# Two layers of attention and a 3x3 convolution: where the positions enter the first attention's scores, when the folded weights are made, and who writes the picture's border

## The chip, the cores and the metric

The kernel runs on one core of a Trainium2 chip. The core has five engines with queues of their own: PE (TensorE: matmuls, with PEld for its weight loads), DVE (VectorE), ACT (ScalarE), POOL (GpSimd) and SP (SyncE, which here only issues transfers). Each engine works through its own instructions in order, and waits where an instruction needs something of another engine. The metric is the device time of one execution in microseconds (us); lower is better.

## The reference, cut to what matters

Two images of 256 channels and 64x64 pixels go through two residual layers, each behind a group normalisation. The first layer is 8-head attention over all 4096 pixels. The second has two attentions over blocks of 64 pixels (`_sa`: one over the 64 pixels that have the same place in their 8x8 blocks, then one within each block), and a 3x3 convolution of mixtures of q, k and v.

```python
x = x + _L0_conv_ref(_gn(x), qkv_w, qkv_b, 8)      # softmax(q k / sqrt(32)) v, 8 heads of 32, N = 4096
x = x + _L1_conv_ref(_gn(x), ...)
...
q = _c1x1(x, conv1_w, conv1_b)
k = _c1x1(x, conv2_w, conv2_b)
v = _c1x1(x, conv3_w, conv3_b)
loc = jnp.stack([linspace over w, linspace over h])
pos = jnp.tile(_c1x1(loc, convp_w, convp_b), (1, HEAD, 1, 1))
fq = q * float(hd) ** (-0.5) + pos
fk = k + pos
...
att = jax.nn.softmax(jnp.einsum('bcn,bcm->bnm', qf, kf) * C ** (-0.5), axis=-1)      # in _sa
...
f_conv = f_all.transpose(0, 2, 1, 3).reshape(b, hd * KC * KC, h, w)
out_conv = lax.conv_general_dilated(f_conv, dep_w, (1, 1), ((1, 1), (1, 1)), feature_group_count=hd, ...)
return rate1 * out_att + rate2 * out_conv
```

The queries and keys of the second layer's first attention are linear in the normalised image and in the pixel's place (its two coordinates and the constant 1). Their scores are therefore a sum of four products: image with image, image with place, place with image, place with place.

## The kernel before

For each image `b` the program runs: load of x, `group_stats`, `project0` (the first layer's projections), `attention0`, `layer1_first` (the second layer's first attention) and `layer1_second` (its second attention and the 3x3). N = 4096 pixels are cut into NT = 8 tiles of T = 512; the 256 channels are KC = 2 halves of 128 partitions.

At the start SP issues the eight loads of x (L70), and behind them 16 loads that put the weights w1 and w2 of the second layer in order of their output channels (`by_out`, L87), and `place_rows` (L91), the four rows of the places' weights. POOL meanwhile issues the loads of the constants, of the first layer's weights (L100 to L135) and of `grid` (L208). `group_stats` takes the statistics with VectorE (L326, L330), and two small matmuls `pm_l` and `pv_l` (L333, L343) spread them over the channels; the first projection `p_wk` (L418) needs them.

`fold_scores` (L213) runs for image 0 behind `project0`. It transposes `place_rows` to `place` (L227), multiplies w1 by w2 to the one matrix `g` of the scores (L238) so that only one projection, y, is needed for queries and keys together, and makes `pos_rows` (rows that add the query's and the key's places to y) and `w_at` (two columns that give, for each pixel, its products with the two coordinates of the key's place).

`attention0` runs through 16 groups of heads and rows in a hand-written order of PE, ACT and DVE: scores (L511), exp (L517), product with the values (L527), sums (L564). Tasks can be hung into it at a group and a step. In image 0's attention nine of them, the list `later`, split the position rows and each tile's places into two parts of reduced precision (`split`: a copy by ACT, L170, and a subtraction by DVE, L171), and store the parts to a DRAM scratch, `loc_kept`.

`layer1_first` regroups the normalised image into `xg`, with tiles in the order of the first small attention. `project` makes `py` with two matmuls for each of 2 x 8 tiles (L1136) and a third of 16 rows that adds the places (L1140); ACT writes the sum to y. `at_grid` makes `pa`, the pixels' products with the coordinates, for four tiles at a time: eight matmuls with `w_at` (L1152) and four with the places (L1154); ACT copies them to `ats` (L1157). `open_pair` loads the places of two tiles from `loc_kept` (L1118). `group_attention` then runs for each tile: `scores` (the products of xg with y, L1031, and a third one of two rows, `ats` with `grid`, L1037), the values (L1013, two halves, written by ACT or DVE), softmax by DVE and ACT (L1045 to L1052), transposes `at` (L1057), copies to a block diagonal `bd` by DVE (L1066), and the output `pc` (L1075), which ACT writes to `feats` (L1086). PE's order here is written by hand: while tile t's scores and values run, tile t-1's softmax is under way, and its `at` and `pc` follow between the halves of the projection of tile t+2. For t of 6 and 7 there is no projection left to lie between.

For image 0, `conv_weights` (L870 to L890) makes the 3x3's weights from the reference's small ones, on VectorE alone, after the first attention's regrouping (`issue_after(done)`): two halves m of 9 taps x 12 combinations (L872) and sums (L876 to L883, the last of them the last weight), each half stored by SP to `wf_kept` (L885). `fetch_conv_weights` loads them as `wf` (L900), and PE transposes them (`pw`, L909).

`layer1_second` pads the picture to 66x66 in `xp`: POOL clears the border (top row L1242, bottom row L1243, left and right columns L1244), and ACT writes the normalised image into the middle (L1248). POOL makes the 3x3's inputs from it in the Winograd form (`conv_transform`: `col` L936 and `v` L940), PE multiplies them (`mm`, L950), and between these steps run the second small attention's `branch` (`phq`, L1290, `prq`, L1298, with ACT's L1086) and `group_attention`.

Of the kernel before, what the change touches and what calls it, by code (L numbers as in the profile page):

```python
# [40 lines left out]
def direct_layers(ctx: ExitStack, tc: tile.TileContext, a: dict, out: bass.AP, bad: bass.AP):  # L41
# [35 lines left out]
    x_first = load_x(0)  # L77
# [13 lines left out]
    nc.sync.dma_start(out=place_rows, in_=a["posq"])  # L91

# [48 lines left out]
    def load_layer1():  # L141
        for name in ("fq2", "fk2"):
            wts[name] = load_const("wt_" + name, [P, KC, C], a[name].rearrange("(k p) m -> p k m", p=P))
        wts["b3"] = load_const("b3", [P, KC], a["b3"].rearrange("(k p) -> p k", p=P))
        wts["rate1"] = load_const("rate1", [P, 1], a["rate1"].partition_broadcast(P))
        wts["rate2"] = load_const("rate2", [P, 1], a["rate2"].partition_broadcast(P))
        def stack(name, rows):
            wts[name] = const.tile([16, rows.shape[1]], F32R, name="st_" + name)
            pair, second = split(rows, name)

            def rest():
                second()
                for g in range(4):
                    nc.sync.dma_start(
                        out=wts[name][4 * g : 4 * g + 4].bitcast(F32), in_=pair[:, g % 2, :].bitcast(F32)
                    )

            return rest

        later.append(lambda: (lambda: stack("pos", wts["pos_rows"])))  # L160


    later = []

    def split(rows, nm):


        n, cols = rows.shape
        pair = w4([n, 2, cols], f"pair_{nm}", F32R)
        nc.scalar.copy(pair[:, 0, :], rows)  # L170
        return pair, lambda: nc.vector.tensor_sub(pair[:, 1, :], rows, pair[:, 0, :].bitcast(F32))  # L171
# [13 lines left out]
    loc_kept = dram.tile([2, 2, 4, N], F32, name="loc_kept")  # L185

    def stack_positions(t):
        n = slice(t * T, (t + 1) * T)
        loc = w4([4, T], f"loc_{t}")
        nc.sync.dma_start(out=loc, in_=a["loc"][:, n])  # L190

        def halves_of():
            pair, second = split(loc, f"loc_{t}")

            def rest():
                second()
                for d in range(2):
                    nc.sync.dma_start(out=loc_kept[:, d, :, n].rearrange("l r n -> r l n"), in_=pair.bitcast(F32))

            return rest  # L200

        return halves_of


    grid = const.tile([P, 64], F32, name="grid")
    nc.gpsimd.memset(grid, 0.0)
    for u in range(4):
        nc.gpsimd.dma_start(out=grid[HD0 * u : HD0 * u + 2, :], in_=a["loc"][1:3, 0:64])  # L208

# [3 lines left out]
    def fold_scores():  # L213
# [3 lines left out]
        rows = w4([4, C + HD0], "pos_rows")  # L217
        wts["pos_rows"] = rows
        nc.gpsimd.memset(rows, 0.0)

        scale = const.tile([4, 1], F32, name="pos_scale")
        nc.gpsimd.memset(scale, 8.0)
        nc.gpsimd.memset(scale[0:1, :], 1.0)
# [5 lines left out]
        pl = bank([4, C + 2], "pt_rows")  # L229
        for dst, src in ((pl[:, 0:C], by_out["w2"]), (pl[:, C : C + 2], place[:, :, 1:3])):  # L230
            for j in range(KC):
                nc.tensor.matmul(dst, place[:, j, :], src[:, j, :], start=j == 0, stop=j == KC - 1)
        nc.scalar.activation(rows[:, 0 : C + 2], pl, AF.Copy, scale=scale)
        for k in range(KC):
            pg = bank([P, C + 2], f"pt_g_{k}")
            for dst, src in ((pg[:, 0:C], by_out["w2"]), (pg[:, C : C + 2], place[:, :, 1:3])):
                for j in range(KC):
                    nc.tensor.matmul(  # L238
                        dst, by_out["w1"][:, j, k * P : (k + 1) * P], src[:, j, :], start=j == 0, stop=j == KC - 1
                    )  # L240
            nc.scalar.copy(wts["g"][:, k, :], pg[:, 0:C])
            nc.scalar.copy(w_at[:, k, 0:2], pg[:, C : C + 2])
# [227 lines left out]
    def attention0(b, xts, held):  # L470
# [253 lines left out]
        rests = {}  # L724
        for n, begin in enumerate(later):
            at_block(1 + n // 2, 3 + 12 * (n % 2), lambda n=n, begin=begin: rests.update({n: begin()}))
            at_block(1 + n // 2, 8 + 12 * (n % 2), lambda n=n: rests.update({n: rests[n]()}))
            at_block(1 + n // 2, 12 + 12 * (n % 2), lambda n=n: rests.pop(n)())
        later.clear()

# [81 lines left out]
    def conv_weights():  # L812
# [49 lines left out]
        for m in range(2):  # L862
# [16 lines left out]
            for r, row in enumerate((g[0], one, two, g[2])):  # L879
# [3 lines left out]
                nc.vector.tensor_add(one, one, row[:, 1, :])  # L883
# [117 lines left out]
    def group_attention(nm, q, k, tokens, wv, out, busy=False, apart=False, more=None):  # L1001
# [25 lines left out]
        for t in range(4):  # L1027
# [7 lines left out]
            for par in range(2 if more else 0):  # L1035
                n0 = (4 * par + t) * 64
                nc.tensor.matmul(  # L1037
                    sp[64 * par : 64 * par + 64, t, :], more[0][:, n0 : n0 + 64], more[1], start=False, stop=True
                )
        if not first:  # L1040
# [50 lines left out]
    def layer1_first(b, xts, put, check, st):  # L1091
# [19 lines left out]
        tiles, banks, locs = {}, {}, {}  # L1111
# [3 lines left out]

        def open_pair(i):
            loc = w4([16, 2, T], f"loc_{b}_{i}", F32R)
            nc.sync.dma_start(  # L1118
                out=loc.bitcast(F32).rearrange("r s n -> r (s n)"),
                in_=loc_kept[:, :, :, 2 * i * T : (2 * i + 2) * T].rearrange("l d r n -> (l d r) n"),  # L1120
            )
            locs[i] = loc

        def loc_of(t):
            return locs[t // 2][:, t % 2, :]
# [813 lines left out]
```

## Time and profile before

| What | us |
|---|---|
| median of three executions (3153.34, 3155.56, 3158.25) | 3155.56 |
| the profiled execution, its own time | 3162.76 |
| its span | 3160.8 |
| start to the first projection (p_wk) | 21.0 |
| projections of image 0, and the fold, to the first scores | 21.0 to 110.5 |
| attention of image 0, to the writing of its last rows | 110.5 to 1153.7 |
| attention of image 1, from its first scores | 1698.1 to 2739.2 |
| second layer of image 0, to the first pw | to 1349.3 |
| second layer of image 1, to its first phq | to 2871.8 |

The profile is of one execution, the one of 3162.76 us in the table. In its lines an instruction group has its start, its duration, the engine (SPq is SP's queue), the line of the code, the operation, the tile written and the tiles read, and in brackets how long the engine had been idle and what ended that. Over the whole span the mean clock that PE was granted is 0.99 of full speed.

### The profile page before, as it was taken

How to read it: one execution, taken by the hardware profiler on the slowest of the kernel's cores; microseconds unless marked ns; L12 is line 12 of the kernel's file. 1: busy time of each engine (PE TensorE's matmuls, PEld its weight loads, DVE VectorE, ACT ScalarE, POOL GpSimd, SP SyncE). 2: the span in 40 equal slices, each digit the busy share in tenths (PEclk: the TensorE clock that was granted, in tenths of full speed). 3: DMA queues.
4: the chain of work that ended last, by engine and by line, in shares of the span. 5: the costliest groups of instructions: out<-in, count | busy, mean ns of one | idle time of the engine just before them, and what ended most of it. 6: DMA issues, size and time to landing. Idle time of an engine off the chain costs nothing. (4 is left out here: it accounts for less than half of the span.)

```text
span 3160.8 us, 62690 instructions
## 1 busy us (share of the span) xinstructions
PE 3059.0 (97%) x25107; PEld 1835.6 (58%) x25107; DVE 2479.1 (78%) x3203; ACT 2302.7 (73%) x2356; POOL 864.9 (27%) x933
## 2 busy tenths in 40 slices
PE   7999999999999999799999999999999999999998
PEld 4455555555555556477654555555555555466765
DVE  4599998999999998846545899899999999824543
ACT  2699999999999973432235999999999999734232
POOL 2122222222322230435301222222222222305530
PEclk9999999999999999899999999999999999999999
DMA  7968778688796661121059686786878975600000
GB/s 257 270 126 171 152 160 179 137 174 167 160 191 134 135 135 49 60 98 36 27 187 271 127 184 141 154 177 143 171 166 164 184 150 125 161 1 8 21 14 22
DMA packets 242709, 425.74 MB, mean 135 GB/s; under 512 B 99164, under 2 KB 109984, under 8 KB 239976
## 3 DMA queue, kind: packets, MB, share of 16 engines
q0 software_dynamic: 96240, 240.41, 38.2%
q1 hardware_dynamic: 146168, 181.24, 20.5%
q8 instruction: 199, 3.26, 0.4%
q14 instruction: 102, 0.84, 0.1%
HBM read 118.52 MB, written 68.12 MB: 59 GB/s over the span
## 5 line engine op out<-in xcount | busy, mean ns | idle before, releaser
L564 DVE TENSOR_TENSOR e<-e,es 128x1024 f32<-128x1024 f32 (+1 forms) x952 | 1035.9, 1143 | 91.4 <-ACT es L517 90.0
L527 PE MATMUL av<-es,v 128*32 128x256 f32 (+1 forms) x9644 | 747.6, 390 | 0.0
L564 DVE TENSOR_TENSOR e<-e,v 128x1024 f32<-128x1024 f32 (+1 forms) x640 | 676.6, 1109 | 51.2 <-ACT v L517 49.8
L517 ACT ACTIVATE es<-sa 128x1536 f32<-128x1536 f32 (+1 forms) x444 | 635.6, 1432 | 97.7 <-PE sa L511 55.0
L511 PE MATMUL sa<-q,k 128*128 128x512 f32 x1736 | 561.6, 431 | 13.6 <-ACT es L517 6.4
L527 PE MATMUL av<-v 128*32 128x256 f32 (+1 forms) x6228 | 507.9, 390 | 0.0
L527 PEld LDWEIGHTS av<-es,v 128*32 128x32 f32 x9644 | 317.0, 110 | 299.9 <-issue 162.1
L511 PEld LDWEIGHTS sa<-q,k 128*128 128x128 f32 x1736 | 280.4, 188 | 296.5 <-issue 138.3
L511 PE MATMUL sc<-q,k 128*128 128x512 f32 x1180 | 372.5, 397 | 4.3 <-ACT es L517 3.3
L511 PE MATMUL sb<-q,k 128*128 128x512 f32 x1180 | 371.2, 396 | 0.8 <-ACT es L517 0.8
L527 PEld LDWEIGHTS av<-v 128*32 128x32 f32 x6228 | 217.5, 110 | 179.4 <-issue 82.7
L517 ACT ACTIVATE es<-sc 128x1024 f32<-128x1024 f32 x296 | 306.8, 1037 | 2.6 <-DMA v<-es 2.6
L517 ACT ACTIVATE v<-sc 128x1024 f32<-128x1024 f32 x294 | 304.8, 1037 | 0.0
L517 ACT ACTIVATE es<-sb 128x1024 f32<-128x1024 f32 x296 | 302.0, 1020 | 2.4 <-DMA acc<-es 2.4
L517 ACT ACTIVATE v<-sb 128x1024 f32<-128x1024 f32 x294 | 299.8, 1020 | 0.0
L511 PEld LDWEIGHTS sc<-q,k 128*128 128x128 f32 x1180 | 211.2, 188 | 74.2 <-ACT es L517 13.1
L511 PEld LDWEIGHTS sb<-q,k 128*128 128x128 f32 x1180 | 221.3, 188 | 55.3 <-ACT es L517 2.8
L574 POOL DMA_DIRECT2D es<-es x118 | 100.7, 853 | 496.3 <-ACT es L517 450.7
L517 ACT ACTIVATE v<-sa 128x1536 f32<-128x1536 f32 (+1 forms) x146 | 209.2, 1433 | 35.3 <-PE sa L511 15.3
L950 PE MATMUL mm<-v,wf 128*128 128x256 f32 x1024 | 229.3, 383 | 4.1 <-DVE z L959 4.1
L940 POOL TENSOR_TENSOR v<-col 128x512 f32<-128x512 f32 x128 | 162.5, 1297 | 228.6 <-PE mm L950 44.0
L950 PEld LDWEIGHTS mm<-v,wf 128*128 128x128 f32 x1024 | 194.9, 191 | 39.4 <-issue 13.5
(258 smaller groups left out, 3240.6 us busy)
## 6 DMA issues: line engine op xcount, KB each, us to landing
acc<-es POOLq DMA_DIRECT2D x130, 512.0 KB, 6.1
acc<-v POOLq DMA_DIRECT2D x84, 512.0 KB, 6.1
es<-es POOLq DMA_DIRECT2D x138, 256.0 KB, 4.0
v<-es POOLq DMA_DIRECT2D x134, 256.0 KB, 4.8
k<-wk_halves SPq DMA_DIRECT2D x64, 512.0 KB
q<-wq_halves SPq DMA_DIRECT2D x256, 128.0 KB
v<-v POOLq DMA_DIRECT2D x90, 256.0 KB, 4.9
es<-v POOLq DMA_DIRECT2D x86, 256.0 KB, 3.8
```

The lines of the kernel that those rows point to most:

```text
L511: nc.tensor.matmul(sc[:, i, :], held["k", g // 2][:, j * P : (j + 1) * P], held["q", g, u // 2][:, u % 2, :], start=True, stop=True,)
L517: nc.scalar.activation(dst, sc[:, i : i + m, :], AF.Exp, scale=SC0)
L527: nc.tensor.matmul(dst[HD0 * u : HD0 * u + HD0, n], lhs, rhs(u)[:, n], start=start, stop=stop)
L564: nc.vector.tensor_add(dst[:, s, :], dst[:, s, :], src)
L574: nc.gpsimd.dma_start(out=dst, in_=src, accum_op=ALU.add)
L940: (nc.gpsimd.tensor_add if plus else nc.gpsimd.tensor_sub)(dst, rows(one), rows(two))
L950: nc.tensor.matmul(mm[:, m, r, :], wf[:, k, 4 * r + q, m * P : (m + 1) * P], v[r // 2][:, r % 2, k, :], start=k == 0, stop=k == KC - 1,)
```

## The change

Five things are changed.

1. The places become three more rows of the scores' third product. `fold_scores` now also makes `query_part` (the three weights of the query's place), `meet` (their product with the key's place), `at_key` (`meet` with `grid`) and a `w_at` of five columns. The third product has five rows for each tile: `queries`, which holds the pixels' products and the raw rows of places, and `keys`, which holds the grid's part and the products with the query's place. `queries` is laid out once in SBUF (`at_query`, cleared by POOL, with eight loads by POOL), stored to `kept_at` by SP, and loaded for each image. `at_grid` loses its four matmuls with the places, and writes with two VectorE combinations instead of ACT's copy. `project` loses its third matmul, and the nine tasks, `loc_kept` and `open_pair` go.
2. `by_out` and `place_rows` are loaded ahead of x, and `fold_scores` runs ahead of `group_stats`.
3. In `group_attention` of the first attention, for t of 6 and 7, the values run after a pause: PE's order is scores(t), at(t-1), values(t), pc(t-1).
4. In `branch` of the first tile the four matmuls run both output halves of the first input half, then those of the second.
5. For image 0 the top row of the picture's border is written by VectorE, issued after the last weight of `conv_weights`. The bottom row and the columns, and image 1's border, stay with POOL.

```diff
-    x_first = load_x(0)
...
     place_rows = const.tile([4, C], F32, name="place_rows")
     nc.sync.dma_start(out=place_rows, in_=a["posq"])
+    x_first = load_x(0)
...
-        later.append(lambda: (lambda: stack("pos", wts["pos_rows"])))
...
-    loc_kept = dram.tile([2, 2, 4, N], F32, name="loc_kept")
-    def stack_positions(t):
...
-    grid = const.tile([P, 64], F32, name="grid")
-    nc.gpsimd.memset(grid, 0.0)
+    AT = 5
+    kept_at = dram.tile([P, 2, T], F32, name="kept_at")
+    at_query = w4([P, 2, T], "at_query")
+    nc.gpsimd.memset(at_query, 0.0)
+    masks = const.tile([P, 2], F32, name="masks")
+    nc.gpsimd.memset(masks, 0.0)
+    grid = const.tile([2, 64], F32, name="grid")
+    nc.gpsimd.dma_start(out=grid, in_=a["loc"][1:3, 0:64])
     for u in range(4):
-        nc.gpsimd.dma_start(out=grid[HD0 * u : HD0 * u + 2, :], in_=a["loc"][1:3, 0:64])
-
+        r = HD0 * u
+        for half in range(2):
+            nc.gpsimd.dma_start(
+                out=at_query[r + 2 : r + AT, half, :], in_=a["loc"][0:3, (4 * half + u) * T : (4 * half + u + 1) * T]
+            )
+        nc.gpsimd.memset(masks[r : r + AT, 1:2], 1.0)
+        nc.gpsimd.memset(masks[r : r + 2, 0:1], 0.125)
+        nc.gpsimd.memset(masks[r : r + 2, 1:2], 0.0)
+    nc.sync.dma_start(out=kept_at, in_=at_query)
+    at_key = const.tile([P, 64], F32, name="at_key")
...
+        part = const.tile([P, KC, 3], F32, name="query_part")
+        for k in range(KC):
+            nc.scalar.activation(
+                part[:, k, 0:1], place[:, k, 0:1], AF.Identity, bias=place[:, k, 3:4], scale=0.125
+            )
+        nc.scalar.copy(part[:, :, 1:3], place[:, :, 1:3])
+
+        def product(dst, lhs, rhs):
             for j in range(KC):
-                nc.tensor.matmul(dst, place[:, j, :], src[:, j, :], start=j == 0, stop=j == KC - 1)
-        nc.scalar.activation(rows[:, 0 : C + 2], pl, AF.Copy, scale=scale)
+                nc.tensor.matmul(dst, lhs(j), rhs(j), start=j == 0, stop=j == KC - 1)
+
+        pm = bank([2, 3], "pt_meet")
+        product(pm, lambda j: place[:, j, 1:3], lambda j: part[:, j, :])
+        meet = const.tile([2, P], F32, name="meet")
+        nc.gpsimd.memset(meet, 0.0)
+        by_four = meet.rearrange("j (u r) -> j u r", u=4)
+        nc.scalar.copy(by_four[:, :, 0:2], ident[0:2, 0:2].unsqueeze(1).to_broadcast([2, 4, 2]))
+        for u in range(4):
+            nc.scalar.copy(by_four[:, u, 2:AT], pm)
+        pk = bank([P, 64], "pt_key")
+        nc.tensor.matmul(pk, meet, grid, start=True, stop=True)
+        nc.scalar.copy(at_key, pk)
         for k in range(KC):
-            pg = bank([P, C + 2], f"pt_g_{k}")
-            for dst, src in ((pg[:, 0:C], by_out["w2"]), (pg[:, C : C + 2], place[:, :, 1:3])):
-                for j in range(KC):
-                    nc.tensor.matmul(
-                        dst, by_out["w1"][:, j, k * P : (k + 1) * P], src[:, j, :], start=j == 0, stop=j == KC - 1
-                    )
+            block = slice(k * P, (k + 1) * P)
+            pg = bank([P, C + AT], f"pt_g_{k}")
+            product(pg[:, 0:C], lambda j: by_out["w1"][:, j, block], lambda j: by_out["w2"][:, j, :])
+            product(pg[:, C : C + 2], lambda j: by_out["w1"][:, j, block], lambda j: place[:, j, 1:3])
+            product(pg[:, C + 2 : C + AT], lambda j: by_out["w2"][:, j, block], lambda j: part[:, j, :])
             nc.scalar.copy(wts["g"][:, k, :], pg[:, 0:C])
-            nc.scalar.copy(w_at[:, k, 0:2], pg[:, C : C + 2])
+            nc.scalar.copy(w_at[:, k, 0:AT], pg[:, C : C + AT])
         nc.sync.dma_start(out=kept_w["g"], in_=wts["g"])
...
-        rests = {}
-        for n, begin in enumerate(later):
...
-                nc.vector.tensor_add(one, one, row[:, 1, :])
+                kept["made"] = nc.vector.tensor_add(one, one, row[:, 1, :])
...
-                    sp[64 * par : 64 * par + 64, t, :], more[0][:, n0 : n0 + 64], more[1], start=False, stop=True
+                    sp[64 * par : 64 * par + 64, t, :], more[0][:, n0 : n0 + 64], more[1][:, n0 : n0 + 64], start=False, stop=True
...
+        if more and more[3]:
+            yield
         if not first:
             values(0)
...
-                nc.tensor.matmul(acc, wts["pos"][:, m * P : (m + 1) * P], loc_of(t), start=False, stop=True)
...
+        queries, keys = cpool.tile([P, 2, T], F32, tag="col", name=f"at_{b}"), {}
+        nc.sync.dma_start(out=queries, in_=kept_at)
 
         def at_grid(half):
             pa = bank([P, T], f"pa_{b}_{half}")
-            for c in range(KC + 1):
+            for c in range(KC):
                 for u in range(4):
-                    t, dst = 4 * half + u, pa[HD0 * u : HD0 * u + HD0, :]
-                    if c < KC:
-                        nc.tensor.matmul(dst, w_at[:, c, :], source(t)[:, c, :], start=c == 0, stop=False)
-                    else:
-                        nc.tensor.matmul(
-                            dst, wts["pos"][:, C : C + HD0].bitcast(F32), loc_of(t).bitcast(F32), start=False, stop=True
-                        )
-            nc.scalar.activation(ats[:, half, :], pa, AF.Copy, scale=0.125)
+                    nc.tensor.matmul(
+                        pa[HD0 * u : HD0 * u + HD0, :], w_at[:, c, :], source(4 * half + u)[:, c, :],
+                        start=c == 0, stop=c == KC - 1,
+                    )
+            keys[half] = w4([P, T], f"keys_{b}_{half}")
+            nc.vector.scalar_tensor_tensor(
+                queries[:, half, :], pa, masks[:, 0:1], queries[:, half, :], ALU.mult, ALU.add
+            )
+            nc.vector.scalar_tensor_tensor(
+                keys[half].rearrange("p (g n) -> p g n", g=8), pa.rearrange("p (g n) -> p g n", g=8), masks[:, 1:2],
+                at_key.unsqueeze(1).to_broadcast([P, 8, 64]), ALU.mult, ALU.add,
...
-                        more=(ats[rows, t // 4, :], grid[rows, :], t == 0),
+                        more=(queries[rows, t // 4, :], keys[t // 4][rows, :], t == 0, t >= NT - 2),
...
+                    if m == 0 and NT - 2 <= t < NT:
+                        next(parts)
...
-            nc.gpsimd.memset(xp[:, k, 0, :], 0.0)
+            if b == 0:
+
+                with tc.issue_after(kept["made"].ins):
+                    nc.vector.memset(xp[:, k, 0, :], 0.0)
+            else:
+                nc.gpsimd.memset(xp[:, k, 0, :], 0.0)
...
-                for m in range(KC):
-                    ph = bank([P, T], f"ph{nm}_{nt}_{m}")
-                    for k in range(KC):
-                        nc.tensor.matmul(
-                            ph, wts[one][:, k, m * P : (m + 1) * P], f[k], start=k == 0, stop=k == KC - 1
-                        )
-                    bn_relu(hid[:, m, :], ph, col1, m)
+                ph = [bank([P, T], f"ph{nm}_{nt}_{m}") for m in range(KC)]
+                for k, m in ((0, 0), (0, 1), (1, 0), (1, 1)) if t == 0 else ((0, 0), (1, 0), (0, 1), (1, 1)):
+                    nc.tensor.matmul(
+                        ph[m], wts[one][:, k, m * P : (m + 1) * P], f[k], start=k == 0, stop=k == KC - 1
+                    )
+                    if k == KC - 1:
+                        bn_relu(hid[:, m, :], ph[m], col1, m)
...
+            if b == 0:
+                fold_scores()
             mean, rstd = group_stats(xts, f"l0_{b}")
...
             held = project0(b, xn, w0)
-            if b == 0:
-                fold_scores()
```

## The prediction

> **What bounds the kernel now.** I read the page's busy times first, then the two attention windows, then, stage by stage, the order in time at the start, at the end of the projections, and in the second layer of each image. TensorE (PE) is busy nearly throughout:
>
> ```profile
> PE 3059.0 (97%) x25107; PEld 1835.6 (58%) x25107; DVE 2479.1 (78%) x3203; ACT 2302.7 (73%) x2356; POOL 864.9 (27%) x933
> ```
>
> What a change is worth is read from its own stage. Four windows (length, busy PE, PEld, DVE, ACT, POOL, granted clock, DMA share, GB/s): the attention of images 0 and 1, then their second layers up to the 3x3's first products.
>
> ```profile
> 110.50:1160.96 1050.46, 1041.58 (x10149) 590.80 (x10149) 960.41 (x986) 978.01 (x932) 280.93 (x342) 1.00 0.77 160
> 1698.10:2746.55 1048.45, 1039.16 (x10148) 590.46 (x10148) 955.44 (x975) 974.84 (x923) 277.37 (x342) 1.00 0.77 160
> 1160.96:1355.00 194.04, 167.55 (x1034) 107.45 (x1035) 157.97 (x396) 82.21 (x118) 57.49 (x35) 0.91 0.21 67
> 2746.55:2880.00 133.45, 121.50 (x810) 77.60 (x811) 38.50 (x89) 59.38 (x79) 19.75 (x21) 0.96 0.10 37
> ```
>
> Image 0's attention is 2.01 us longer than image 1's; the nine position tasks (on ACT, DVE and SP) exist only in the former. In image 0's second layer DVE is busy 157.97 of 194 us (it makes the 3x3's weights); in image 1's PE is, 121.50 of 133.45. So matmuls removed from the second layer are paid in image 1 alone.
>
> The start, in order of time (start, duration, engine, idle before and releaser):
>
> ```profile
> 0.74 4.20 SPq L70 DMA_DIRECT2D x<-in_x_dram  x8
> 4.98 13.71 SPq L87 DMA_DIRECT2D w_by_out<-in_wx_dram  x16
> 16.52 0.59 PE L333 MATMUL pm_l<-mv_l,group 128*128 128x2 f32 x2 [16.52 <-DVE mv_l L330]
> 21.01 15.51 PE L418 MATMUL p_wk<-xn,wqk 128*128 128x512 f32 x32 [2.48 <-DVE xn L368]
> 19.37 2.17 POOL L135 DMA_DIRECT2D bv_last<-in_bv_dram  x4
> 22.23 2.02 POOL L208 DMA_DIRECT2D grid<-in_loc_dram  x4
> 107.22 1.13 PE L238 MATMUL pt_g<-w_by_out 128*128 128x256 f32 x4
> ```
>
> Image data alone lead to the first projection at 21.01; the fold's products run at 105, when their weights have long been there.
>
> **Part 1, the fold "while x loads": a loss.** Three steps. (a) x is queued behind 16 weight loads and place_rows: 17 x 0.42 = 7.1 us (the median issue of L87 is 0.419 us; the row's 13.71 us is stretched by x's traffic), so the statistics could be ready at 16.5 + 7.1 = 23.6, or some 24.4 as the weights share the load. (b) But PE runs in program order, the fold now stands ahead of pm_l, and the fold's pt_key waits for ACT's meet, which waits for POOL's memset of meet. On POOL that memset stands behind the memset of at_query (twice bd's 0.55 us, 1.1), the grid load, eight position loads and the masks. POOL ends bv_last at 21.5 now; less the waits that come from x's early traffic, 18.5 to 20, plus 1.1: the grid is issued at some 20.5. Eight loads at 0.5 (L208: 2.02/4) to 0.9 us (the slow ones, L122) and the small memsets: 6.5 us, so meet at about 27 (25.5 to 30). (c) Then ACT's copies and pt_key 1.4, and the pt_g products: 107.22 to 109.95 now, 2.7, plus eight 128x3 products at the 128x2 ones' 0.13 us, 1.0: the fold leaves PE at about 32.8 (30.5 to 36) with some 0.7 for ACT between. pm_l to p_wk takes 21.01 - 16.52 = 4.5 us, less the ACT table load of 1.28 us between them, which no longer waits for PE: 3.3. First projection at 36.2 instead of 21.0: **+15.2** (13 to 18.5). At the end of the projections the fold is gone: last p_wq to first exp is 7.5 us in image 0 (105.35 to 112.85) and 3.54 in image 1 (1695.87 to 1699.41), **-4.0**.
>
> **Part 2, the nine tasks.** First scores to the writing of the last rows: 1043.13 against 1041.06 us: **-2.1** (0 to 2.1).
>
> **Part 3, image 0's second layer.** DVE's chain of weights ends it (tile names as in the code):
>
> ```profile
> 1288.88 22.44 POOL L936 TENSOR_TENSOR col<-xp 128x1152 f32<-128x1152 f32 x1 [7.05 <-ACT xp L1248]
> 1309.25 2.36 DVE L872 SCALAR_TENSOR_TENSOR prep<-prep 128x256 f32<-128x256 f32 x1
> 1331.07 1.09 DVE L883 TENSOR_TENSOR prep<-prep 128x256 f32<-128x256 f32 x3
> 1333.22 0.69 PE L1057 MATMUL at_sr<-ident,e_sr 128*128 128x128 f32 x2 [17.75 <-DVE e_sr L1052]
> 1336.97 0.33 SPq L900 DMA_DIRECT2D wf<-wf_kept  x1
> 1349.30 1.97 PE L909 MATMUL pw<-ident,wf 128*128 128x128 f32 x16
> ```
>
> POOL's first transform takes 22.44 us where the later ones take 2.1 to 2.2, and from 1309.25 on DVE's operations take 1.1 to 2.4 us instead of 0.4. The fourteen from 1309.25 to 1327.66 would take 5.4 us at the pitch of their like elsewhere (0.40 for L872, 0.34, 0.2 for L984, 0.87 for L876): 13.0 us lost while POOL transforms. With the border written by DVE after the last weight, POOL has no complete picture until DVE is done, so the two no longer meet: -13.0. DVE gains four 128x512 combinations (0.75 us each, the L424 row): 3.0, partly inside the 3.82 us that L870 waits for its load at 1261; I take +1.5 (0 to 3.0). Behind the last weight come its store, the load of wf (issued at 1336.97, traffic to about 1348.2) and pw. That load is late next: 16.0 us after the weights, wherever they end; PE's own work to pw, 12.2 us from the pc at 1337.11, is ready earlier. Now pw starts 1.1 us after wf has landed, as PE is late too; that goes: -1.1. Sum **-12.6** (9 to 16). POOL loses its head start of three transforms, but the first four v operations take 5 us and wf's load is longer. PE's savings here (as in part 4) lie under DVE's chain.
>
> [...]
>
> **Part 4, image 1's second layer, PE bound.**
>
> ```profile
> 2831.14 0.50 PE L1140 MATMUL py<-loc,st_pos 16*128 16x512 f32 x1
> 2854.33 2.02 PE L1075 MATMUL pc_lr<-bd,vs_lr 128*128 128x128 f32 x16 [1.42 <-DVE bd L1066]
> 2871.78 3.70 PE L1290 MATMUL phq_sr<-feats,wt_fq 128*128 128x512 f32 x8 [2.23 <-ACT feats L1086]
> ```
>
> L1140 goes: 16 at 0.43 us start to start, -6.9. L1154 goes: two times 1.0 (1231.56 to 1232.56), -2.0. The third scores product keeps its columns, five rows instead of two: nothing. With the values behind the next step, the 1.42 us above and its twin of 1.44 us before the next pc are covered by a values block of 1.9 us: -2.6 after a restart. The order of phq lets four matmuls run on the first feats: 4 x 0.43, of which I count -1.5 (ACT is busy there with the picture). VectorE's combinations instead of ACT's copy lie behind values; if that cover were gone they would cost 0.75 each. POOL's transforms may take 0.5 back. **-12.5** (10 to 13.5).
>
> **Sum.** +15.2 - 4.0 - 2.1 - 12.6 - 12.5 = -16.0. The profiled execution took 3162.76 us (span 3160.8 and 2 around it), 7.2 above the median of 3155.56; none of these stages explains that, so the sum is set against the median: 3139.5, say **3140 us**. Its own range by the bounds above is 3132 to 3147.
>
> **Rivals.** *The fold hides while x loads.* For it: weights and place_rows would be there by some 12 us. Then only x's 7.1, less the table load's 1.3, and -4.0: 9.4 better, 3130. Against: POOL reaches meet only after the x load. *The move of the border gains nothing,* since the load of wf or POOL's late transforms take the chain over: 0 to 3 instead of 12.6, 3149 to 3152. For it: wf's load follows 1.1 us behind; POOL has then done no transform when PE asks. Against: PE waited 17.75 us for e_sr, all of it DVE. *Slower: POOL's loads at the start run one after another,* each waiting for the one before to land (4.5 to 5.2 us for a small load under x's traffic): nine at 5.3 instead of 0.7 put meet some 41 us later; -16 + 41 gives 3181. It decides from 22 us of further delay (16.0 + 6.3). For it: POOL waits for landed loads at 7.69, 8.64 and 13.04. Against: four grid loads went out in 2.02 us.
>
> **How the numbers follow.** The forecast has 0.58, the hidden fold 0.07, the idle border 0.22, POOL's chain 0.13. No change is within 0.2%, 6.3 us, which a measurement of this kernel can hardly tell: 3149.2 to 3161.9. Faster: 0.55 of the forecast, all of 0.07 and 0.09 of the idle border, 0.71. Same: 0.03 + 0.12 + 0.01 = 0.16. Slower: the rest, 0.13. The range of 8 in 10 reaches over the idle border, and to the hidden fold's edge: 3126 to 3155.
>
> **What would show it.** The first p_wk at 34 to 40, its idle before ended by the fold's chain and POOL's meet at 25 to 30; the last p_wq to first exp near 3.5 in image 0; its attention at 1041 us; POOL's first L936 near 2.2 us and DVE at 0.4 through the last weights, pw 16 us after them; no stall of 1.4 before image 1's pc. A first p_wk under 30, or a pw that waits for POOL, would prove me wrong.

## The result, and the profile after

| | median us | executions |
|---|---|---|
| before | 3158.47 | 18 |
| changed | 3151.38 | 18 |

The ratio is 0.9975, with a 95% interval of 0.9968 to 0.9982: 7.9 us shorter (0.0025 x 3158), 5.7 to 10.1 by the interval; the two medians themselves differ by 7.1. The forecast was 16 us shorter, so the direction was right and the size half. The profiled execution of the changed kernel took 3150.88 us, its span 3149.1; its profile is 11.7 us shorter than that of before, which had caught an execution 4 us above its median.

The stages, worked out from the starts of the first instruction of each kind in the traces (us; "exp" the first exponential, "rows" the writing of the attention's last rows, "mm" the first product of the 3x3, "phq" the first product of the second small attention, "tail" from there to the span's end). The kernels named in the lower rows are described with their experiments:

| kernel | first p_wk | p_wk to exp 0 | attention 0, exp to rows | rows to mm, image 0 | mm to exp 1 | attention 1 | rows to phq, image 1 | tail |
|---|---|---|---|---|---|---|---|---|
| before | 21.0 | 91.8 | 1040.8 | 203.6 | 342.2 | 1039.8 | 132.6 | 289.0 |
| changed | 39.4 | 89.1 | 1041.1 | 187.4 | 342.4 | 1041.7 | 118.3 | 289.8 |
| border by POOL | 39.4 | 89.0 | 1040.5 | 197.3 | 343.4 | 1042.5 | 118.3 | 291.6 |
| fold behind | 21.9 | 97.0 | 1036.0 | 184.3 | 342.1 | 1042.0 | 118.3 | 293.4 |
| meet early | 32.0 | 88.3 | 1040.3 | 187.4 | 342.5 | 1041.6 | 118.3 | 290.3 |
| two queues | 28.5 | 89.2 | 1040.4 | 188.0 | 342.5 | 1042.5 | 118.3 | 292.6 |
| before with border | 21.5 | 91.8 | 1038.4 | 192.4 | 342.2 | 1039.2 | 132.6 | 288.9 |
| aligned | 39.4 | 89.2 | 1039.0 | 185.2 | 343.3 | 1037.9 | 118.3 | 289.9 |
| before shifted | 21.3 | 92.4 | 1040.0 | 201.1 | 342.5 | 1042.0 | 132.6 | 291.0 |
| among | 20.5 | 93.5 | 1042.4 | 184.6 | 342.3 | 1037.4 | 118.3 | 289.7 |

The busy times of the changed kernel, from its page, show that PE is still the bound, with 20 us less work:

```profile
PE 3039.4 (97%) x25049; PEld 1831.2 (58%) x25049; DVE 2472.8 (79%) x3204; ACT 2298.8 (73%) x2352; POOL 845.7 (27%) x947
```

The start of the changed kernel, from its timeline:

```profile
0.74 7.36 SPq L86 DMA_DIRECT2D w_by_out<-in_wx_dram  x16
8.56 4.89 SPq L70 DMA_DIRECT2D x<-in_x_dram  x9
28.08 0.19 POOL L209 MEMSET meet<- 2x128 f32 x1
28.31 0.20 ACT L211 COPY meet<-ident 2x8 f32<-2x8 f32 x1 [17.48 <-POOL meet L209]
28.82 0.66 PE L215 MATMUL pt_key<-grid,meet 2*128 2x64 f32 x2 [17.69 <-DMA at_query<-in_loc_dram]
29.40 2.08 PE L204 MATMUL pt_g<-w_by_out 128*128 128x256 f32 x4
36.25 0.57 PE L315 MATMUL pm_l<-mv_l,group 128*128 128x2 f32 x2
39.38 2.93 PE L400 MATMUL p_wk<-xn,wqk 128*128 128x512 f32 x3 [1.13 <-DVE xn L350]
```

x is issued from 8.56 on. PE waits 17.69 us at pt_key, the fold's first product with meet; the bracket names a load of at_query, but pt_key reads meet, which ACT writes only after POOL's memset at 28.08. The fold itself takes from 28.8 to 36.2 us: four of its 128x256 products take 2.08 us, where before, behind the projections, they took 1.13. What the order of the queue costs is seen in the windows of the first 10 us (busy PE, PEld, DVE, ACT, POOL, granted clock, DMA share, GB/s), here of the kernel before:

```profile
0.00:5.00 5.00, 0.00 (x0) 0.00 (x0) 0.61 (x1) 0.00 (x0) 4.01 (x13) 1.00 0.63 205
5.00:10.00 5.00, 0.00 (x0) 0.00 (x0) 3.92 (x8) 0.00 (x0) 3.15 (x8) 1.00 1.05 396
```

and here of the changed one:

```profile
0.00:5.00 5.00, 0.00 (x0) 0.00 (x0) 0.00 (x0) 1.28 (x1) 4.01 (x13) 1.00 0.22 62
5.00:10.00 5.00, 0.31 (x2) 0.28 (x2) 0.00 (x0) 0.00 (x0) 5.00 (x12) 1.00 0.32 64
```

Sixteen loads of 32 KB keep SP's queue busy and the transfer engines mostly idle (shares of 0.22 and 0.32), at 62 to 64 GB/s.

The second layer of image 0 in the changed kernel, from its timeline:

```profile
1325.15 0.69 PE L1034 MATMUL at_sr<-ident,e_sr 128*128 128x128 f32 x2 [9.00 <-DVE e_sr L1029]
1331.58 2.13 POOL L911 TENSOR_TENSOR col<-xp 128x1152 f32<-128x1152 f32 x1 [47.17 <-DVE xp L1213]
1335.95 0.33 SPq L875 DMA_DIRECT2D wf<-wf_kept  x1
1348.19 8.87 PE L884 MATMUL pw<-ident,wf 128*128 128x128 f32 x64 [2.90 <-DMA wf<-wf_kept]
```

POOL's first transform takes 2.13 us instead of 22.44, PE's wait for e_sr has gone from 17.75 to 9.00, and pw now waits for the load of wf, as the forecast had it.

The second layer of image 1, from its timeline:

```profile
2839.44 0.44 PE L1034 MATMUL at_lr<-ident,e_lr 128*128 128x128 f32 x2
2839.72 3.62 PE L988 MATMUL pvs_lr<-wt_w,xg 128*128 128x256 f32 x16
2843.17 1.95 PE L1052 MATMUL pc_lr<-bd,vs_lr 128*128 128x128 f32 x16
2859.26 3.70 PE L1262 MATMUL phq_sr<-feats,wt_fq 128*128 128x512 f32 x8 [2.69 <-ACT feats L1063]
```

The values stand between at and pc, and the wait of 1.4 us before pc is gone.

### The profile page after: what moved, and what is told of

Read it like the earlier page. It is cut to its first block, busy times and chain, and to the rows that moved or that the text cites. A ratio compares the mean times of both kernels' runs of the same rounds, so it can differ in the third digit from the quotient of the medians.

```text
span 3149.1 us, 62530 instructions
## 1 busy us (share of the span) xinstructions
PE 3039.4 (97%) x25049; PEld 1831.2 (58%) x25049; DVE 2472.8 (79%) x3204; ACT 2298.8 (73%) x2352; POOL 845.7 (27%) x947
## 3 DMA queue, kind: packets, MB, share of 16 engines
q1 hardware_dynamic: 146056, 181.94, 21.3%
## 5 line engine op out<-in xcount | busy, mean ns | idle before, releaser
L925 PEld LDWEIGHTS mm<-v,wf 128*128 128x128 f32 x1024 | 194.5, 191 | 39.7 <-issue 13.3
```

The source lines that it names most:

```text
L925: nc.tensor.matmul(mm[:, m, r, :], wf[:, k, 4 * r + q, m * P : (m + 1) * P], v[r // 2][:, r % 2, k, :], start=k == 0, stop=k == KC - 1,)
```

## Experiments

All ratios are to the kernel before on the same chip in the same rounds; with the kernel before near 3160 us, 0.0010 is 3.2 us. The changed kernel stands at 0.9975.

**The border by POOL again.**

```diff
-            if b == 0:
-                with tc.issue_after(kept["made"].ins):
-                    nc.vector.memset(xp[:, k, 0, :], 0.0)
-            else:
-                nc.gpsimd.memset(xp[:, k, 0, :], 0.0)
+            nc.gpsimd.memset(xp[:, k, 0, :], 0.0)
```

> The changed kernel with one part undone: the top border row of image 0's picture is cleared by POOL again. Theory (the border's move is worth what its stage shows, about 16 us from the attention's last rows to the first product of the 3x3): POOL's first col takes over 15 us again, DVE's operations are stretched to 1 to 2.4 us behind it, the last weight moves from 1331 to about 1345 and the time goes up by 13 to 16 us, to about 3165, at or above the kernel before. Rival (the gain lies elsewhere, in the fewer matmuls): up by less than 5.

1.0009 [1.0000, 1.0018], 10.7 us more than the changed kernel (0.0034 x 3160, give or take 4 by the two intervals): nearer the theory than the rival, but less than its 13 to 16. POOL and DVE hold each other up again (28.96 us instead of 2.13 for the transform, 2.37 instead of 0.4 for a combination), in the timeline of this kernel:

```profile
1290.39 28.96 POOL L911 TENSOR_TENSOR col<-xp 128x1152 f32<-128x1152 f32 x1 [8.03 <-ACT xp L1216]
1317.27 2.37 DVE L847 SCALAR_TENSOR_TENSOR prep<-prep 128x256 f32<-128x256 f32 x1
```

From image 0's last rows to the first mm it needs 197.3 us, 9.9 more than the changed kernel and 6.3 less than the kernel before. So 6 us of that stretch came without the border.

**The border alone, in the kernel before.** The edit is the five lines above, and `kept["made"] =` ahead of the last sum.

> The kernel before with the changed kernel's border alone: the top row of image 0's picture is cleared by VectorE after the last weight. The undoing of it in the changed kernel lengthened the stretch from image 0's last rows to the first product of the 3x3 by 9.9 us. Theory (the move is worth the same here, and the other 6 us of that stretch come from the positions): the stretch falls from 203.6 to about 193, the last weight comes 10 to 13 us earlier, the time is 9 to 12 us shorter than the kernel before. Rival (the two parts only work together, since PE's later at_sr holds the stretch): under 5 us. The attention of image 1, 1039.8 us in the profile of before and 1041.6 to 1042.5 in those of all changed kernels, shows here whether it belongs to the kernel or to the execution: near 1040 if the former.

0.9966 [0.9955, 0.9977], again 10.7 us, and the stretch falls from 203.6 to 192.4. The move is worth the same with and without the rest. Image 1's attention is at 1039.2, like before.

**x first, the fold behind the projections.** Part 2 of the change undone.

```diff
+    x_first = load_x(0)
     by_out = {}
...
     nc.sync.dma_start(out=place_rows, in_=a["posq"])
-    x_first = load_x(0)
...
-            if b == 0:
-                fold_scores()
             mean, rstd = group_stats(xts, f"l0_{b}")
...
             held = project0(b, xn, w0)
+            if b == 0:
+                fold_scores()
```

> The changed kernel with its second part undone: x is loaded first and the fold runs behind the projections; the positions stay as five rows. Theory (the early fold cost the start 18 us and gave 4 back): first p_wk at 21 again, a gap of 5 to 7 us between the last projection and the first exp, so the first exp at 114 to 117 instead of 128.4, and the time 11 to 14 us shorter than the changed kernel, near 3138 to 3140. Rival (the start's loss is made up later, in the attention): less than 5 us shorter.

0.9937 [0.9923, 0.9950], 12.0 us shorter than the changed kernel, as the theory had it: part 2 is a loss. First p_wk at 21.9; the gap behind the projections is larger than expected (first exp at 118.8). Its timeline shows where:

```profile
108.85 0.24 PE L204 MATMUL pt_meet<-query_part,place 128*2 128x3 f32 x4 [1.79 <-ACT query_part L200]
109.86 1.13 PE L204 MATMUL pt_g<-w_by_out 128*128 128x256 f32 x4
111.72 2.06 PE L204 MATMUL pt_g<-w_by_out 128*128 128x256 f32 x4
```

PE waits 1.79 us for ACT, and some 3 us later, from 111.72 us on, the same four products take 2.06 us instead of 1.13.

**meet and the grid's load at the head of POOL's queue.**

```diff
     nc.gpsimd.memset(eps, 1e-5)
+    meet = const.tile([2, P], F32, name="meet")
+    nc.gpsimd.memset(meet, 0.0)
+    grid = const.tile([2, 64], F32, name="grid")
+    nc.gpsimd.dma_start(out=grid, in_=a["loc"][1:3, 0:64])
```

> The changed kernel, but POOL clears meet and issues the grid's load right behind ident and eps, ahead of its other loads; the weights stay ahead of x. Theory (POOL's order held the fold, and a cold PE stretched it): the fold runs at 11 to 18 us while x loads, pm_l follows the statistics at 28.4 and the first p_wk starts at 31 to 32 instead of 39.4: 7 to 8 us shorter, near 3144. What is left of the start's loss, 10 us, is x's later arrival. Rival (the weights' products wait for their loads under x's traffic, POOL did not matter): first p_wk stays over 37, less than 2 us.

0.9951 [0.9937, 0.9964], 7.6 us shorter than the changed kernel. Its timeline:

```profile
11.92 0.68 PE L215 MATMUL pt_key<-grid,meet 2*128 2x64 f32 x2 [0.40 <-ACT meet L213]
28.87 0.59 PE L315 MATMUL pm_l<-mv_l,group 128*128 128x2 f32 x2 [9.35 <-DVE mv_l L312]
```

Now the fold does run while x loads, and PE then waits 9.35 us for the statistics. So of the 12 us that part 2 costs, 7 to 8 were the fold's place behind POOL's queue.

**x on one queue, the weights on another.** The previous edit, x first, and `nc.scalar.dma_start` for the 17 loads.

> The kernel of the previous run with x first on SP's queue and the 17 loads of the weights and place_rows on ACT's queue, which is idle then. Theory (the loss is one of queues: x stood behind 17 issues while the transfers ran at a sixth of their rate): x lands as in the kernel before, the statistics end at 16 to 18, the fold is done by then or soon after, the first p_wk starts at 21 to 24, and there is no fold behind the projections: 15 to 18 us shorter than the changed kernel, 3134 to 3137. Rival (transfers are shared, so weights beside x come as late as behind it and hold pm_l): first p_wk at 27 or later, 8 to 12 us.

0.9947 [0.9934, 0.9961]: 8.8 us shorter than the changed kernel, and the rival was right. Its timeline:

```profile
16.04 0.34 PE L194 MATMUL pt_place<-ident,place_rows 4*128 4x4 f32 x2 [16.04 <-DMA place_rows<-in_posq_dram]
25.34 0.57 PE L315 MATMUL pm_l<-mv_l,group 128*128 128x2 f32 x2
```

place_rows, the last of the 17, lands at 16.0 under x's traffic, the fold then takes 9.3 us, and pm_l stands behind it. So in these runs the fold stays on the path ahead of the statistics unless its data come before x, as in the run before.

**Idle products to bring PE to full pace.** 64 products of ident by ident, into a bank that nothing reads, ahead of pt_key.

> The changed kernel with 64 idle products of 128x128 (ident by ident, into a bank of their own that nothing reads) between pt_meet and pt_key, where PE waits 17.7 us for POOL's meet. Theory (PE's first work after a rest runs at half pace, which stretched the fold's products from 3.7 to 7.0 us and is the error of the start's term): with the idle products ending shortly before meet is there, a product of 128x256 takes 0.28 instead of 0.52 us, the fold ends 2 to 3.5 us earlier, and so does the first p_wk. If they end too early (64 at half pace are 64 x 0.2 or so, 13 us from 11 to 24, and 4 us before meet), part of it is lost. Rival (the slow products have another cause, such as the loads that run beside them): no change in the fold's own duration.

The first p_wk stays at 40.0. The windows of this kernel (granted clock third from the right) cover the idle products, twice, and the fold, twice:

```profile
11.30:13.30 2.00, 2.00 (x11) 2.00 (x10) 0.78 (x2) 0.00 (x0) 2.00 (x3) 1.00 1.05 382
15.30:17.30 2.00, 2.00 (x21) 2.00 (x20) 1.29 (x2) 0.00 (x0) 1.65 (x3) 1.00 1.10 309
30.30:33.30 3.00, 3.00 (x14) 2.77 (x14) 0.00 (x0) 0.21 (x1) 2.71 (x5) 0.68 0.69 198
33.30:36.80 3.50, 3.50 (x14) 3.14 (x14) 0.00 (x0) 0.44 (x2) 0.00 (x0) 0.50 0.37 131
```

The idle products go from 11 to 21 in 2 us: PE began at half pace and sped up, though both windows read a clock of 1.00. They ended 3.0 us before pt_key. In the fold the granted clock reads 0.68 from 30.3 to 33.3 us and 0.50 from 33.3 to 36.8, and the four 128x256 products take first 1.38, then 2.05 us. Meet came at 29.6 us here, 1.5 later than in the changed kernel. So the slow products of the fold go with the granted clock here; that full pace would save the 3 us was not shown, since it did not last. The ratio, 0.9951 [0.9936, 0.9966], is of four executions and lower than any stage of this profile explains; I leave it open. It is 7.6 us below the changed kernel's, a warning of how far a single comparison of ratios can be trusted here.

**The order of the values (part 3) and of the branch (part 4), each undone.**

> The changed kernel with the values of the two last tiles of the first small attention back behind their own scores (part 3 undone). Theory: image 1's PE stalls before pc return, 1.4 us twice, and the stretch from image 1's last rows to its first phq grows from 118.3 by 2.6 to 2.9 us; image 0's stretch is unchanged within 0.5. Rival: other engines' waits take their place, under 1 us.

Image 1's stretch from rows to phq is 121.3, 3.0 more; the stalls are back in the timeline:

```profile
2844.67 2.02 PE L1052 MATMUL pc_lr<-bd,vs_lr 128*128 128x128 f32 x16 [1.42 <-DVE bd L1043]
2854.56 2.02 PE L1052 MATMUL pc_lr<-bd,vs_lr 128*128 128x128 f32 x16 [1.44 <-DVE bd L1043]
```

> The changed kernel with the four matmuls of the first branch in their old order (part 4 undone). phq starts when the first feats are there in the changed kernel, so its start should not move much; the order shows in what follows. Theory: with the old order the second half's matmuls come later by 1.5 us, and the first mm of image 1 after phq comes 1 to 1.7 us later. Rival: feats' second half is there before the third matmul either way, no difference over 0.3 us.

No gain from part 4: phq starts at the same distance from the rows (118.3) and the first mm follows 6.97 us behind it, 7.30 in the changed kernel. The rival was right; when phq starts, both halves of feats are there. (The times of these two, of one execution each, are not compared.)

**The places of the tiles.** In the profiles of the changed kernels DMA is busier than before for the same bytes, and image 1's attention, whose code is the same, is longer. The change replaced some of the small constant tiles by others, and all large tiles, which lie behind the constants in SBUF, moved 352 bytes down: from a multiple of 256 bytes to 160 past one. (This is reckoned from the tiles in the code; the traces name no addresses.) The edit restores the old places:

```diff
+    pad = const.tile([P, 88], F32, name="pad")
+    nc.gpsimd.memset(pad, 0.0)
     ident = const.tile([P, P], F32, name="ident")
```

> The changed kernel with an unused tile of 88 numbers per partition among the constants, so that the large tiles lie at the same places in SBUF as before (the changed list of constants had moved them all by 352 bytes, from a multiple of 256 bytes to 32 bytes past a multiple of 128). In the profiles of all changed kernels the attentions' adding DMAs take longer than before (acc from es 6.4 against 6.0 us, es from es 4.5 against 3.8 to 3.9) and image 1's attention, whose code is the same, is 1.0 to 4.1 us longer. Theory (the places do it): the DMAs are back at 6.0 and 3.8, image 1's attention at 1039 to 1040, image 0's at 1037 to 1039 (its nine tasks are gone), the time 3 to 6 us shorter. Rival (the order of the work ring or chance does it): DMAs at 6.4 as now, no difference.

0.9942 [0.9929, 0.9955]: 10.4 us shorter than the changed kernel (give or take 5 by the two intervals), more than the theory's 3 to 6. And the reverse, a tile of 40 numbers in the kernel before:

> The kernel before with an unused tile of 40 numbers per partition among the constants, which puts the large tiles 32 bytes past a multiple of 128, as the change did. Theory (the places slow the attentions' DMAs): acc from es at 6.4 us instead of 6.0, both attentions 1 to 3 us longer, the time 2 to 5 us longer. Rival: no difference over 1 us and DMAs at 6.0.

1.0024 [1.0015, 1.0032]: 7.6 us longer than before, also more than expected. The lines of the DMA queue that POOL issues (packets, MB, share of 16 engines) and of one adding transfer (count, KB, us to landing), before:

```profile
q0 software_dynamic: 96240, 240.41, 38.2%
acc<-es POOLq DMA_DIRECT2D x130, 512.0 KB, 6.1
```

the kernel before, shifted:

```profile
q0 software_dynamic: 96240, 240.41, 39.6%
acc<-es POOLq DMA_DIRECT2D x130, 512.0 KB, 6.4
```

changed:

```profile
q0 software_dynamic: 96400, 240.46, 39.8%
acc<-es POOLq DMA_DIRECT2D x130, 512.0 KB, 6.4
```

changed, aligned:

```profile
q0 software_dynamic: 96400, 240.46, 38.4%
acc<-es POOLq DMA_DIRECT2D x130, 512.0 KB, 6.1
```

The share goes with the places in all fifteen profiles: 38.2 to 38.6% in the four kernels with the old places, 39.6 to 39.9% in the eleven others. The same bytes cost 4% more engine time. So does image 1's attention, whose code no run changes: 1037.4 to 1039.8 us in the four, 1040.8 to 1043.9 in the eleven. Two more pads tell whether it is the remainder or the added tile, and which unit counts: 32 numbers (the tiles lie 32 bytes past a multiple of 256) and 8 numbers (192 past one).

> The changed kernel with an unused tile of 32 numbers (128 bytes per partition): the large tiles move, but stay 32 bytes past a multiple of 128. Theory (what counts is the remainder, not the tile that was added or its clearing by POOL): no gain, within 2.5 us of the changed kernel (ratio to before near 0.9975), the share of POOL's DMA queue near 39.7%. Rival (any shift, or the added clearing, brings the gain of the aligned version): 3140 to 3147, share near 38.4%.

> The changed kernel with an unused tile of 8 numbers (32 bytes per partition): the large tiles lie 64 bytes past a multiple of 128, a multiple of 64 but not of 128. Theory (64 bytes are the unit): the whole gain of the aligned version, a ratio to before near 0.994 and a share of POOL's DMA queue near 38.4%. Rival (128 or 256 bytes are the unit): near the changed kernel, 0.9975 and 39.7%.

0.9976 [0.9967, 0.9986] and 0.9969 [0.9957, 0.9981], with shares of 39.7% and 39.9%: neither has the gain. So it is not the added tile, and a multiple of 64 is not enough; a multiple of 256 is. A multiple of 128 that is not one of 256 was not tried.

Taken together, 0 bytes past a multiple of 256 gives shares of 38.2 to 38.6%, while 160, 32 and 192 past it give 39.6 to 39.9%. What causes the difference the runs do not show.

**A version of what was learnt.** x first, the large tiles at their old places, and `fold_scores` as a generator whose five steps stand among the projections:

```diff
         heads4("wk0", 0)
+        next(fold, None)
         heads4("wq0", 0)
         for i in range(N // P // 4):
...
             nc.sync.dma_start(out=vals[b][:, 4 * i : 4 * i + 4, :], in_=st)
+            next(fold, None)
```

with a `yield` behind query_part, behind meet, and ahead of each of the two pt_g.

> A version put together from what the runs showed: the changed kernel with x loaded first, the fold cut into five steps among the projections (after the first group of wk, after wq's, and behind the first three groups of the values), where PE is the bound and no wait of ACT is left to it, and the large tiles back at their old places. Expected: first p_wk at 21 to 22, first exp 5 to 8 us earlier than with the fold behind the projections less its own products of 3.7 to 4.5 us, so at 113 to 115; attentions at 1038 to 1040 each; 18 to 24 us shorter than the changed kernel, 3128 to 3134. If the places have no effect, 4 us more; if the steps make PE wait for ACT, first exp at 117 or later.

0.9914 [0.9901, 0.9927]: 27 us shorter than the kernel before, 19 shorter than the changed one; median 3134.4. Its timeline:

```profile
20.46 16.23 PE L405 MATMUL p_wk<-xn,wqk 128*128 128x512 f32 x32 [2.48 <-DVE xn L355]
61.95 1.03 PE L207 MATMUL pt_g<-w_by_out 128*128 128x256 f32 x4
112.63 0.93 PE L500 MATMUL sa<-q,k 128*128 128x512 f32 x3 [2.27 <-issue]
```

No product of the fold waits here, and pt_g runs at full pace, 1.03 us. First exp is at 113.9 us, as expected and 4.9 earlier than with the fold behind the projections; image 0's attention, 1042.4, is longer than expected.

What the pieces themselves are worth is not shown by the ratio: x first (12.0) and the old places (10.4) add up to 22 us, and this kernel, which has both, gained 19. With 4 to 5 us of uncertainty in each, the 4.9 us of the profile can be neither confirmed nor excluded. A kernel with x first, the fold behind and the old places was not run.

## Why the prediction was half right

Measured by ratios, the forecast's parts without the places give 18.3 us (the aligned kernel), where it said 16; the places took 10.4 of them back. That 18.3 is so near 16 is partly luck: in the changed kernel's profile the start and the gap behind the projections cost 4.6 us more than said, and the two second layers gave 5.4 more. The sum's own range is also added up wrongly: its bounds reach from 4.5 to 22.6 us shorter, so to 3133 and 3151 us, not 3132 and 3147. Point by point:

- **The step that failed is the sum itself**, "+15.2 - 4.0 - 2.1 - 12.6 - 12.5 = -16.0": it took all that the change does not name as unchanged, the attentions above all, with 2080 of the 3160 us. A term of about +10 us was missing, the slower transfers from the moved tiles (10.4 us in the changed kernel, 7.6 in the kernel before). None of the three rivals had it, and the diff shows it only as a changed list of small tiles. Over the fifteen profiles, image 1's attention is on average 3.7 us longer with the moved places and the tail 1.7; image 0's attention (1036.0 to 1043.7 us) and its stretch to mm do not separate the two groups. The rest could not be placed.
- **The start**, +15.2: the mechanism was right, the size was +18.4. Meet came at 28.1 (27 was said). The terms that were mis-sized are the fold's products, 6.8 us at half pace instead of 3.7 and 0.7, and x, whose statistics came at 28.4 instead of 24.4. The latter did not count beside meet. **The gap behind the projections** is 2.6 to 2.8 us smaller, not 4.0.
- **The nine tasks**, -2.1: not seen. Image 0's attention is 1038.4 to 1042.4 us in the four profiles with aligned tiles, with and without tasks. A gain of 2 us cannot be told from this spread, and it stays open.
- **Image 0's second layer**, -12.6: -16.2 in the changed kernel, -18.4 aligned; the profiles with this part of the change lie between -15.6 and -19.5, whatever the places. The border is worth 10.7, close to the 13.0 - 1.5 said for it. What was wrong is that PE's savings here "lie under DVE's chain": the rest of the change gave 6. DVE waits for the load of the second half of the weights at the same distance from the rows (107.8 and 108.4 us), but behind that wait it has one softmax of the first small attention left instead of two, and two pairs of copies to bd instead of four, as PE has got further. The load of wf is late next, as said. After the move POOL's transforms cost DVE's softmax little: of its five steps at 1345.34 to 1348.41 us, one took 1.04 us instead of 0.42.
- **Image 1's second layer**, -12.5: -14.3. L1140 was taken at 0.43 us, start to start; a tile's period fell from 12.86 to 11.65 us, 0.6 for each of two. The values' order gave 3.0 (2.6 said), the branch's order nothing (1.5 said). That POOL's transforms take 0.5 us back is shown by no run; from the rows to phq it is 132.6 us before and 118.3 in the changed kernel.
- **The rivals.** The hidden fold is what the change does not have and the early meet does. The idle border is refuted twice, by the two runs on the border. POOL's loads one after another did not happen: eight went out between 22.2 and 27.0.

## What to carry to other kernels

A diff that adds or drops a small tile can move the tiles behind it, here by 352 bytes as reckoned from the code; where transfers are as busy as here (a DMA share of 0.77 to 0.80 in the attentions), compare the DMA queues' share for the same bytes before reading anything else, and try the large tiles on multiples of 256 bytes. "While x loads" is only true of what needs nothing from a queue that x or its neighbours fill: follow every operand of the moved step to its issue, the smallest memset included (meet's takes 0.19 us, and came at 28.08). Work that must be done once can go in pieces inside a stage whose engine is the bound: the fold's products ran at full pace there (1.03 us for four of 128x256) and waited for nothing, while the same fold ran at half pace ahead of the stage (2.08), and in its second half behind it (2.06). How much that is worth in the whole kernel is not settled here.

## What the runs showed of the hardware

- Large tiles 160, 32 or 192 bytes past a multiple of 256 cost 4% more DMA time for the same bytes, and some 8 to 10 us of 3160, in a kernel whose transfers are busy 0.77 to 0.80 of its attentions.
- PE's products after a rest at the start ran at half pace (2.08 us for four of 128x256 behind a wait of 17.7 us, 1.03 to 1.13 among or right behind other work) while the window's granted clock read 1.00. With the idle products, behind a rest of 3.0 us, the same pace (2.05 us for four) came with a reading of 0.50. Why the reading differs is not shown. With the fold behind the projections PE rested for 1.8 us, and the second four took 2.06 us.
- One POOL operation that started during DVE's chain of combinations on prep took 22.4 and 29.0 us instead of 2.1. DVE kept its 0.40 us a piece until 1309.25 (kernel before) and 1317.27 us (border by POOL); there one combination took 2.4 us, about as long as POOL's operation takes undisturbed, and POOL's ended with it, within 0.3 us. From then on DVE's operations on 128x256 of prep took 1.1 to 2.4 us instead of 0.4, beside POOL's next ones. What held POOL's operation until then, and why it ended there, is not shown.
